# Query and key of a decoder layer's self-attention by seven half-size products, and row normalisation on ScalarE

## The chip, the core and the metric

The kernel runs on one core of a Trainium2 chip. The core has five engines with instruction queues of their own: TensorE (PE: matmuls and transposes; PEld are its weight loads), VectorE (DVE), ScalarE (ACT), GpSimd (POOL) and SyncE (SP, which issues most DMAs). Each takes its instructions in the order in which the compiler has put them; semaphores make one wait for another. The metric is the device time of one execution in microseconds (us). The kernel before took 2171.88 us, the median of three runs (2171.53 to 2173.71).

## What is computed

One decoder layer in float32, on x of 16 batches with 128 tokens (rows) and 1024 channels:

```python
x = x + self_attention(layernorm(x), Wqkv, bqkv, Wo, bo)
x = x + cross_attention(layernorm(x), ctx, ctx, Wq, Wk, Wv, Wo, bo, g)
x = x + ffn(layernorm(x), int4 weights of gate, up and down with scales and zeros)

# the part that the change touches, for each batch:
qkv = layernorm(x) @ Wqkv + bqkv             # 1024 -> q, k, v of 256 each
a = softmax(q @ k.T / sqrt(256))             # 128 x 128
x = x + (a @ v) @ Wo + bo
```

## The kernel before, in words

The program has three stages, one after the other: self-attention, cross-attention and the feed-forward network. The change lies in the first, which takes the first 250 of 2171 us. While that stage runs, DVE also prepares weights of the third: `prepare` (line 222 ff.) is a generator, named `early`, that unpacks four-bit numbers, subtracts zeros, multiplies by scales, forms sums of quarters, and has POOL issue the stores. Each `next(early)` emits one step of it; a job (one block of one matrix) is three steps, and the twelve jobs of this stage are 36 steps.

**Groups.** Self-attention works on four groups (`t` = 0 to 3) of four batches, 512 tokens each. Per group:
- *Rows.* `row_stats` (means and variances, DVE, line 144), `row_rstd` (add on DVE, power on POOL, line 150), then `turn` (line 389) for each batch: normalise 128 rows of 1024 channels (DVE, line 156), eight PE transposes into two PSUM banks (line 386), and copies into `xnT` (channels on partitions, 8 chunks of 128 channels by 512 tokens), one half by DVE (line 393), one by ACT (line 394). A group's rows are turned while the group before it multiplies. The first group's go through `first_rows`, with the normalisation on ACT already (line 169).
- *Query and key.* `query_key` (line 436): four output tiles `f` of 128 features (two of query, two of key); each is 8 matmuls, one for each chunk of channels, of 128x128 weights with 512 tokens (line 441), and ACT adds the bias on the way to `qkT` (line 450). The first group does each tile in two halves of 256 tokens.
- *Values.* `value` (line 452): for each batch, 8 matmuls of 128 tokens by 256 features (line 456), bias added by DVE (line 463).
- *Weights.* `weigh`: scores (line 471), maximum on DVE (line 479), exponentials on ACT (line 484), division on DVE (492, 493); `turn_weights`: four transposes and a copy on ACT (501, 503); `attend` (511, 514) gives `oT`.
- *Give.* For a batch of the group before, `oT` times `Wo` (line 335), added to the row `X[b]` by DVE (line 342), and the row's statistics for the next stage. `add_bias` (line 433) adds `bo` to `X[b]` on POOL.

**Order.** In the loop over `t`, each query/key tile is followed by `add_bias`, a `give`, a `turn` for the next group and one or two `next(early)`. After the four tiles come value 0, `weigh`, the other values with `turn_weights` between them, `attend`, and up to four more `next(early)`. A scheduler may let an instruction overtake others of its engine when it deems it ready. An engine wrapped in `InOrder` (line 72; its instructions all show as line 80) pins each of its instructions behind everything that was written before it on that engine; the preparation's DVE work is pinned so, other DVE work is not. In the trace, row statistics of the third group run at 31 us, long before their place in the text.

**Buffers.** PSUM: five banks named `mm` for products, three named `tr` for transposes. SBUF pools: `a_w` for weights, `a_1` with one buffer for each name, `a_2` with two (`xnT`, `xn`, `qkT`, `v`). The next stage's first loads (lines 688 to 713) wait on SP for the buffers of this stage and of the preparation.

Of the kernel before, what the change touches and what calls it, by code (L numbers as in the profile page):

```python
# [12 lines left out]
F32 = mybir.dt.float32  # L13
I32 = mybir.dt.int32
AF = mybir.ActivationFunctionType
ALU = mybir.AluOpType
# [3 lines left out]
P = 128  # L20
B, S, C = 16, 128, 1024
DH = C // 4
# [5 lines left out]
CC = C // P  # L28
NB = C // P
TB = 512  # L30
BPT = TB // S
# [52 lines left out]
def decoder_layer(  # L84
# [70 lines left out]
    def normalise(dst, src, b):  # L155
        nc.vector.tensor_scalar(
            dst, src, mv[:, b, 0:1], rstd[:, b : b + 1], ALU.subtract, ALU.mult
        )


    shift = stat.tile([P, B], F32, name="shift")

    def row_shift(b, vector):
        vector.scalar_tensor_tensor(
            shift[:, b : b + 1], mv[:, b, 0:1], -1.0, rstd[:, b : b + 1], ALU.mult, ALU.mult
        )
# [188 lines left out]
    with (  # L355
# [27 lines left out]
        def turn_half(xn, xnT, b, h):  # L383
            tr = atr.tile([P, 4, P], F32, name="tr")
            for j in range(4):
                nc.tensor.transpose(tr[:, j, :], xn[:, ts(4 * h + j, P)], ident)  # L386
            return xnT[:, ts(h, 4), ts(b % BPT, S)], tr

        def turn(b, xnT):

            xn = a2.tile([P, C], F32, name="xn")
            normalise(xn, X[b], b)
            nc.vector.tensor_copy(*turn_half(xn, xnT, b, 0))
            nc.scalar.copy(*turn_half(xn, xnT, b, 1))

        def first_rows(xnT):

            vector = InOrder(tc, nc.vector)
            halves = {}

            parts = {}

            def half(b, h):
                if h == 0:
                    parts[b] = small.tile([P, 2, 6], F32, name="bnst")
                vector.bn_stats(parts[b][:, h, :], X[b][:, ts(h, 512)])
                if h == 1:
                    vector.bn_aggr(mv[:, b, :], parts[b])
                    row_rstd(b, 1, vector)

            def rows(b):
                xn = a2.tile([P, C], F32, name="xn")
                row_shift(b, vector)
                normalise_act(xn, X[b], b)
                halves[b] = turn_half(xn, xnT, b, 0)
                nc.scalar.copy(*turn_half(xn, xnT, b, 1))

            def copy(b):
# [12 lines left out]
            copy(BPT - 1)  # L431

        def add_bias(b):
            nc.gpsimd.tensor_tensor(X[b], X[b], bo_sb, ALU.add)

        def query_key(f, xnT, qkT, ps=None, tokens=slice(None)):

            if ps is None:
                ps = aps.tile([P, TB], F32, name="mm")
            for c in range(CC):  # L440
                nc.tensor.matmul(  # L441
                    ps[:, tokens],
                    wqkv_sb[:, f, c, :],
                    xnT[:, c, tokens],
                    start=(c == 0),
                    stop=(c == CC - 1),
                )
            if tokens == ts(0, TB // 2):
                return
            nc.scalar.activation(qkT[:, f, :], ps, AF.Identity, bias=bqk_sb[:, f : f + 1])  # L450

        def value(i, xnT, v):

            ps = aps.tile([P, DH], F32, name="mm")
            for c in range(CC):
                nc.tensor.matmul(  # L456
                    ps,
                    xnT[:, c, ts(i, S)],
                    wqkv_sb[:, 4:6, c, :],
                    start=(c == 0),  # L460
                    stop=(c == CC - 1),
                )
            nc.vector.tensor_tensor(v[:, i, :], ps, bv_sb, ALU.add)

        def weigh(qkT):

            scale = 1.0 / math.sqrt(DH)
            ps = aps.tile([P, BPT, S], F32, name="mm")
            for i in range(BPT):
                for d in range(2):  # L470
                    nc.tensor.matmul(  # L471
                        ps[:, i, :],
                        qkT[:, d, ts(i, S)],
                        qkT[:, 2 + d, ts(i, S)],
                        start=(d == 0),
                        stop=(d == 1),
                    )
            nmax = small.tile([P, BPT], F32, name="nmax")
            nc.vector.tensor_reduce(nmax, ps, AX.X, ALU.max, negate=True)
            nc.scalar.mul(nmax, nmax, scale)  # L480
            at = a1.tile([P, BPT, S], F32, name="at")
            den = small.tile([P, BPT], F32, name="den")
            for i in range(BPT):
                nc.scalar.activation(
                    at[:, i, :],
                    ps[:, i, :],
                    AF.Exp,
                    bias=nmax[:, i : i + 1],
                    scale=scale,
                    accum_out=den[:, i : i + 1],  # L490
                )
            nc.vector.reciprocal(den, den)
            nc.vector.tensor_tensor(
                at, at, den.unsqueeze(2).to_broadcast([P, BPT, S]), ALU.mult
            )
            return at

        def turn_weights(at):
            tr = atr.tile([P, BPT, S], F32, name="tr")
            for i in range(BPT):  # L500
                nc.tensor.transpose(tr[:, i, :], at[:, i, :], ident)
            atT = a1.tile([P, BPT, S], F32, name="atT")
            nc.scalar.copy(atT, tr)
            return atT
# [17 lines left out]

        xnTs = [a2.tile([P, CC, TB], F32, name="xnT")]
        first_rows(xnTs[0])
        oT = None
        for t in range(NT):
            xnT = xnTs.pop()
            more = t + 1 < NT
            if more:
                xnTs.append(a2.tile([P, CC, TB], F32, name="xnT"))  # L530
                for b in range((t + 1) * BPT, (t + 2) * BPT):
                    row_stats(b)
                row_rstd((t + 1) * BPT, BPT)
            qkT = a2.tile([P, 4, TB], F32, name="qkT")
            halves = {}
            if t == 0:

                for f in range(4):
                    halves[f] = aps.tile([P, TB], F32, name="mm")
                    query_key(f, xnT, qkT, halves[f], ts(0, TB // 2))  # L540
            for f in range(4):
                if t == 0:
                    query_key(f, xnT, qkT, halves[f], ts(1, TB // 2))
                else:
                    query_key(f, xnT, qkT)
# [8 lines left out]
            v = a2.tile([P, BPT, DH], F32, name="v")  # L554
            value(0, xnT, v)
            at = weigh(qkT)
            if more:
# [4 lines left out]
                if t == 0:  # L562
                    for _ in range(3):
                        next(early)
            else:

                for i in range(1, BPT):
                    give((t - 1) * BPT + i - 1, oT)
                    value(i, xnT, v)
                    next(early, None)  # L570
                atT = turn_weights(at)
                give(t * BPT - 1, oT)
            oT = attend(atT, v)
            for _ in range((3, 3, 4, 0)[t]):
                next(early, None)
    for _ in early:
        pass
    first.close()
# [1477 lines left out]
```

## Time and profile before

| what | value |
|---|---|
| median of three runs | 2171.88 us |
| the profiled execution's own time | 2173.11 us |
| its span (first to last instruction) | 2171.3 us |
| granted TensorE clock | 0.999 of full |
| PE's share of the chain that ended last | 95% |
| first group's matmuls | from 12.55 us |
| start of group t = 1, t = 2, t = 3 | 65.47, 128.66, 191.36 us |
| first key matmul of cross-attention | 250.38 us |
| DMA while self-attention runs (0 to 300 us) | 173 GB/s |

The profile is that of one execution. A row of a timeline has the start, the length, the engine, the line, the operation, the tiles written and read, the shape and the number of instructions merged in it; behind it in brackets stands how long the engine was idle before and which operation released it. Durations of neighbours on one engine overlap a little, so that the distance from start to start is the better price of an operation in a run of them. A float32 matmul shows as two PE instructions. A row by stage has the stretch in microseconds, its length, the busy time and number of instructions of PE, PEld, DVE, ACT and POOL, the granted clock, the DMA share and GB/s. A row of waits has who waited for whom, the total, the number and the longest.

### The profile page before, as it was taken

Reading aid. Unit: us, or ns where it says so; the run is one execution under the profiler, and the core shown is the slowest. Engines: PE = TensorE matmul, PEld = TensorE weight load, DVE = VectorE, ACT = ScalarE, POOL = GpSimd, SP = SyncE. Lnnn points to the kernel's source line nnn. Section 1 sums busy time; section 2 is a strip of 40 time slices with the busy share of each in tenths; the row PEclk is TensorE's granted clock in tenths of the full one; section 3 lists DMA queues with packets and bytes.
Section 4 is the critical chain, followed back from the end, with each engine's and each line's share of the span. In section 5 each row is a group of like instructions: output and inputs, shape, how many; then the busy total and the mean of one; then the engine's idle time right before and its main releaser. Section 6 shows DMA issues by size and latency. Waiting matters only on the chain.

```text
span 2171.3 us, 25688 instructions
## 1 busy us (share of the span) xinstructions
PE 2153.8 (99%) x9004; PEld 1643.8 (76%) x9004; DVE 1556.3 (72%) x2098; ACT 525.5 (24%) x710; POOL 803.9 (37%) x675
## 2 busy tenths in 40 slices
PE   8999999999999999999999999999999999999998
PEld 7565655555555568888888888888886888888887
DVE  7899578888888758786777987878774445534573
ACT  2111235655665541211221212112111000000000
POOL 5454124333433345544444545444441022323200
PEclk9999999999999999999999999999999999999999
DMA  6446447777797676878888746677667578979941
GB/s 259 150 131 219 154 136 237 236 226 236 223 276 242 191 237 217 288 254 262 264 282 290 228 150 209 209 238 237 201 206 237 182 206 242 282 197 254 265 128 60
DMA packets 272203, 474.56 MB, mean 219 GB/s; under 512 B 29633, under 2 KB 128321, under 8 KB 266177
## 3 DMA queue, kind: packets, MB, share of 16 engines
q1 hardware_dynamic: 226736, 383.02, 54.6%
q0 software_dynamic: 27456, 71.45, 12.1%
q10 hardware_dynamic: 17872, 18.36, 2.6%
q8 instruction: 74, 1.21, 0.2%
q14 instruction: 65, 0.52, 0.1%
HBM read 314.64 MB, written 157.55 MB: 217 GB/s over the span
## 4 chain that ended last, share of the span: by engine, by line
PE 95%; DVE 3%; issue 1%; ACT 0%; POOL 0%; DMA 0%; DVEq 0%; POOLq 0%; ACTq 0%
PE q L80 38%; PE po L1929 22%; PE kq L80 10%; PE mm L80 8%; PE kx L80 5%; PE mm L441 4%; PE p L80 3%; PE mm L456 2%; PE mm L335 1%; DVE pa L80 1%; PE tr L386 0%; DVE C L80 0%; DVE pc L80 0%; PE mm L471 0%; PE mm L511 0%
## 5 line engine op out<-in xcount | busy, mean ns | idle before, releaser
L80 PE MATMUL q<-ti,li 128*128 128x256 f32 x1680 | 385.4, 379 | 0.0
L80 PEld LDWEIGHTS q<-ti,li 128*128 128x128 f32 x1680 | 319.2, 190 | 43.4
L80 ACT COPY k<-q 128x512 f32<-128x512 f32 x210 | 122.9, 585 | 660.7 <-PE q L80 645.7
L80 POOL TENSOR_TENSOR li<-w 128x512 f32<-128x512 f32 x140 | 203.8, 1461 | 52.2 <-PE q L80 31.6
L872 POOL TENSOR_TENSOR qe<-qe,qrec 128x1024 f32<-128x1024 f32 x64 | 146.2, 2284 | 175.2 <-DVE qrec L80 156.6
L80 POOL TENSOR_TENSOR li<-w,li 128x512 f32<-128x512 f32 x70 | 107.9, 1541 | 259.5 <-PE q L80 235.5
L1929 PE MATMUL po<-wc,lc 128*128 128x256 f32 x840 | 183.4, 379 | 0.0
L1929 PEld LDWEIGHTS po<-wc,lc 128*128 128x128 f32 x840 | 159.6, 190 | 21.8
L80 DVE TENSOR_TENSOR C<-q,k 128x512 f32<-128x512 f32 x150 | 102.7, 685 | 70.2 <-PE q L80 65.8
L80 PE MATMUL q<-b,w 128*128 128x256 f32 x640 | 151.2, 379 | 0.0
L80 POOL TENSOR_TENSOR li<-li,w 128x512 f32<-128x512 f32 x70 | 91.6, 1309 | 122.2 <-PE q L80 121.8
L80 PEld LDWEIGHTS q<-b,w 128*128 128x128 f32 x640 | 121.6, 190 | 17.0 <-issue 0.5
L80 PE MATMUL q<-ti,w 128*128 128x256 f32 x560 | 132.3, 379 | 0.0
L1929 PE MATMUL po<-wq,lq 128*128 128x256 f32 x560 | 126.8, 379 | 0.8 <-DVE m L80 0.8
L80 PEld LDWEIGHTS mm<-qs,m_sb 128*128 128x128 f32 x512 | 97.3, 190 | 40.1 <-issue 29.7
L80 PE MATMUL kx<-ek,cxt 128*128 128x512 f32 x256 | 121.8, 598 | 0.0
L80 DVE STREAM_TRANSPOSE kt<-qe 128x1024 f32<-128x1024 f32 x64 | 79.2, 1238 | 58.8 <-POOL qe L872 54.6
L80 PE MATMUL mm<-qs,m_sb 128*128 128x256 f32 x512 | 120.8, 379 | 0.0
L80 PE MATMUL kq<-wq_sb,xn 128*128 128x512 f32 x256 | 120.2, 593 | 0.4 <-ACT qe L860 0.4
L80 PE MATMUL kq<-wk_sb,cx 128*128 128x512 f32 x256 | 120.1, 592 | 0.0
L1929 PEld LDWEIGHTS po<-wq,lq 128*128 128x128 f32 x560 | 106.0, 190 | 16.7 <-DVE m L80 1.2
L80 DVE TENSOR_TENSOR pa<-pa,sz 128x1024 f32<-128x1024 int32 x86 | 116.4, 1354 | 2.1
(203 smaller groups left out, 3712.2 us busy)
## 6 DMA issues: line engine op xcount, KB each, us to landing
ti<-r SPq DMA_DIRECT2D x36, 1024.0 KB, 7.4
w<-wg SPq DMA_DIRECT2D x140, 256.0 KB, 3.3
w<-wu SPq DMA_DIRECT2D x140, 256.0 KB, 3.8
lq<-h SPq DMA_DIRECT2D x140, 256.0 KB, 5.3
kd<-kt SPq DMA_DIRECT2D x62, 512.0 KB, 3.7
qs<-kd SPq DMA_DIRECT2D x244, 128.0 KB, 3.2
h<-h SPq DMA_DIRECT2D x80, 256.0 KB, 3.1
wq<-wd SPq DMA_DIRECT2D x70, 256.0 KB, 7.4
```

What stands on the lines that cost most here:

```text
L80: return lambda *args, **kw: self._tc.keep_in_program_order(fn(*args, **kw))
L335: tensor.matmul(ps, oT[:, d, ts(b % BPT, S)], wo_d[d][:, ts(h, 512)], start=(d == 0), stop=(d == 1),)
L441: nc.tensor.matmul(ps[:, tokens], wqkv_sb[:, f, c, :], xnT[:, c, tokens], start=(c == 0), stop=(c == CC - 1),)
L456: nc.tensor.matmul(ps, xnT[:, c, ts(i, S)], wqkv_sb[:, 4:6, c, :], start=(c == 0), stop=(c == CC - 1),)
L872: nc.gpsimd.tensor_tensor(qe, qe, rec.unsqueeze(2).to_broadcast(wide), ALU.mult)
L1929: nc.tensor.matmul(bank[:, i, :], l[:, ts(i, S)], w,  start=(start and c == 0 and i % 2 == 0), stop=(stop and c == len(pairs) - 1), skip_g ...
```

## The change

*Seven products.* For the second to fourth group, the product of query/key weights and rows is cut in two along output features (query, key), channels (chunks 0 to 3, 4 to 7) and tokens (256 and 256). Eight products of quarters are replaced by seven of sums and differences of quarters (the Winograd form of Strassen's method). `weight_sums` makes three sums of weight quarters (S1, S2, S4) once, in the first group, and overwrites a fourth quarter by a difference: four DVE operations of 128x1024, pinned in order. For each group, DVE makes the differences of tokens T1, T2, T3 and a second form of T2, four of 128x1024; T3 overwrites a quarter of `xnT` (in the last group it has a tile of its own). Products 6, 5 and 3 are added on top of product 1 in its PSUM bank, and product 4 on top of product 7. Between, ACT copies partial sums with the bias to `qkT` (8 of 128x256 in place of 4 of 128x512), and DVE adds three of 128x512.

*Order.* Values of batches 2 and 3 come ahead of the products (value 0 too), value 1 after them. Two of the four pieces of work for the neighbouring groups (`beside`) go between products, two after `weigh`; in the last group all four go between products. The steps of `early` by group are 5, 10, 10, 11 in place of 6, 9, 12, 9.

*Rows.* `turn` normalises on ACT (which needs `shift`, made for four batches in one DVE instruction) and copies both halves on ACT. Row statistics are written one group earlier.

*Buffers.* `qkT` and `v` have one buffer; the softmax's tile shares one with T1; S1, S2 and S4 are new.

The diff, cut to its core:

```diff
     def turn(b, xnT):
         xn = a2.tile([P, C], F32, name="xn")
-        normalise(xn, X[b], b)
-        nc.vector.tensor_copy(*turn_half(xn, xnT, b, 0))
-        nc.scalar.copy(*turn_half(xn, xnT, b, 1))
+        normalise_act(xn, X[b], b)
+        for h in range(2):
+            nc.scalar.copy(*turn_half(xn, xnT, b, h))
...
-            at = a1.tile([P, BPT, S], F32, name="at")
+            at = a1.tile([P, 2 * BPT, S], F32, name="T1")[:, :BPT]
...
+        HALF, HC = TB // 2, CC // 2
+        S1, S2, S4 = (aw.tile([P, 2, HC, P], F32, name=f"S{n}") for n in (1, 2, 4))
+        def outputs_by_inputs(m, kc):
+            return wqkv_sb[:, ts(m, 2), ts(kc, HC)]
+        def weight_sums():
+            A = outputs_by_inputs
+            for dst, a, b, op in (
+                (S1, A(1, 0), A(1, 1), ALU.add),
+                (S2, S1, A(0, 0), ALU.subtract),
+                (S4, A(0, 1), S2, ALU.subtract),
+                (A(1, 0), A(0, 0), A(1, 0), ALU.subtract),
+            ):
+                InOrder(tc, nc.vector).tensor_tensor(dst, a, b, op)
+        def query_key_products(xnT, qkT, own=None):
+            A = outputs_by_inputs
+            def rows(kc, th):
+                return xnT[:, ts(kc, HC), ts(th, HALF)]
+            T1 = a1.tile([P, 2 * BPT, S], F32, name="T1").rearrange("p (c h) s -> p c (h s)", c=HC)
+            T2 = a1.tile([P, HC, HALF], F32, name="T2")
+            T3 = rows(0, 1) if own is None else own
+            nc.vector.tensor_tensor(T1, rows(0, 1), rows(0, 0), ALU.subtract)
+            nc.vector.tensor_tensor(T2, rows(1, 1), T1, ALU.subtract)
+            L = {1: A(0, 0), 2: A(0, 1), 4: A(1, 1), 7: A(1, 0), 5: S1, 6: S2, 3: S4}
+            R = {1: rows(0, 0), 2: rows(1, 0), 3: rows(1, 1), 4: T2, 5: T1, 6: T2, 7: T3}
+            bank = {}
+            def biased(m, th, ps):
+                for n in range(2):
+                    f = 2 * m + n
+                    nc.scalar.activation(
+                        qkT[:, f, ts(th, HALF)], ps[:, n], AF.Identity, bias=bqk_sb[:, f : f + 1]
+                    )
+            def add(m, th, ps):
+                dst = qkT[:, ts(m, 2), ts(th, HALF)]
+                nc.vector.tensor_tensor(dst, ps, dst, ALU.add)
+            def third():
+                nc.vector.tensor_tensor(T3, rows(1, 1), rows(0, 1), ALU.subtract)
+            def product(p):
+                first = {6: 1, 5: 1, 3: 1, 4: 7}.get(p, p)
+                if p == first:
+                    bank[p] = aps.tile([P, 2, HALF], F32, name="mm")
+                ps = bank[first]
+                for n in range(2):
+                    for c in range(HC):
+                        nc.tensor.matmul(
+                            ps[:, n],
+                            L[p][:, n, c],
+                            R[p][:, c],
+                            start=(p == first and n == c == 0),
+                            stop=(p in (2, 3, 4) and c == HC - 1),
+                            skip_group_check=True,
+                        )
+                if p == 1:
+                    biased(0, 0, ps)
+                elif p == 7:
+                    biased(1, 1, ps)
+                elif p == 6:
+                    biased(1, 0, ps)
+                    nc.vector.tensor_tensor(T2, rows(1, 0), T2, ALU.subtract)
+                elif p == 2:
+                    add(0, 0, ps)
+                elif p == 5:
+                    add(1, 1, ps)
+                elif p == 4:
+                    add(1, 0, ps)
+                else:
+                    biased(0, 1, ps)
...
+            def beside(f, between=lambda: None):
                 add_bias(t * BPT + f)
+                if t + 2 < NT:
+                    row_stats((t + 2) * BPT + f)
                 if more:
                     if oT is not None:
                         give((t - 1) * BPT + f, oT)
+                    between()
                     turn((t + 1) * BPT + f, xnTs[0])
                 if t > 0:
-                    for _ in range(2 if t == 2 else 1 + f % 2):
+                    for _ in range((3, 2, 2, 2)[f] if more else 2):
                         next(early, None)
...
+            else:
+                for i in (2, 3) if more else ():
+                    value(i, xnT, v)
+                third()
+                value(0, xnT, v)
+                for f, ps in enumerate(((1, 7), (6, 2), (5, 4), (3,))):
+                    for p in ps:
+                        product(p)
+                    if f < 2 or not more:
+                        beside(f)
+                    elif f == 2:
+                        next(early)
+                value(1, xnT, v)
+                at = weigh(qkT)
+                if more:
+                    beside(2)
+                    turned = []
+                    beside(3, lambda: turned.append(turn_weights(at)))
+                    atT = turned.pop()
```

More of the change, by code (lines that the diff above doesn't have):

```diff
@@ L153, in row_rstd, with row_shift @@
         gpsimd.tensor_tensor(r, r, mhalf[:, :n], ALU.pow)
[L155 to L158, printed above, removed]
     shift = stat.tile([P, B], F32, name="shift")
[L163 removed]
+    def row_shift(b, vector, n=1):
         vector.scalar_tensor_tensor(
[L165 removed]
+            shift[:, b : b + n], mv[:, b : b + n, 0], -1.0, rstd[:, b : b + n], ALU.mult, ALU.mult
         )
@@ new lines, in query_key_products @@
+        def query_key_products(xnT, qkT, own=None):
[51 more added lines that the diff above has]
+                    biased(0, 1, ps)
+            return product, third
@@ L528, in decoder_layer @@
             more = t + 1 < NT
+            qkT = a1.tile([P, 4, TB], F32, name="qkT")
+            if t > 0:
+                own = None
+                if not more:
+                    own = a2.tile([P, CC, TB], F32, name="xnT")[:, :HC, :HALF]
+                product, third = query_key_products(xnT, qkT, own)
             if more:
                 xnTs.append(a2.tile([P, CC, TB], F32, name="xnT"))
-                for b in range((t + 1) * BPT, (t + 2) * BPT):
+                for b in range(BPT, 2 * BPT) if t == 0 else ():
                     row_stats(b)
                 row_rstd((t + 1) * BPT, BPT)
[L534 to L545, printed above, removed]
+                row_shift((t + 1) * BPT, nc.vector, BPT)
+            def beside(f, between=lambda: None):
                 add_bias(t * BPT + f)
+                if t + 2 < NT:
+                    row_stats((t + 2) * BPT + f)
                 if more:
@@ L549, in decoder_layer @@
                         give((t - 1) * BPT + f, oT)
+                    between()
                     turn((t + 1) * BPT + f, xnTs[0])
                 if t > 0:
-                    for _ in range(2 if t == 2 else 1 + f % 2):
+                    for _ in range((3, 2, 2, 2)[f] if more else 2):
                         next(early, None)
[L554 to L557, printed above, removed]
+            v = a1.tile([P, BPT, DH], F32, name="v")
+            if t == 0:
+                halves = {}
+                for f in range(4):
+                    halves[f] = aps.tile([P, TB], F32, name="mm")
+                    query_key(f, xnT, qkT, halves[f], ts(0, HALF))
+                for f in range(4):
+                    query_key(f, xnT, qkT, halves[f], ts(1, HALF))
+                    beside(f)
+                value(0, xnT, v)
+                at = weigh(qkT)
+                weight_sums()
                 value(1, xnT, v)
@@ L561, in decoder_layer @@
                 value(3, xnT, v)
-                if t == 0:
-                    for _ in range(3):
-                        next(early)
[L565 to L572, printed above, removed]
+                for _ in range(3):
+                    next(early)
[3 more added lines that the diff above has]
+                third()
+                value(0, xnT, v)
+                for f, ps in enumerate(((1, 7), (6, 2), (5, 4), (3,))):
+                    for p in ps:
+                        product(p)
+                    if f < 2 or not more:
+                        beside(f)
+                    elif f == 2:
+                        next(early)
+                value(1, xnT, v)
+                at = weigh(qkT)
+                if more:
[3 more added lines that the diff above has]
+                    atT = turned.pop()
+                else:
+                    for i in range(1, BPT):
+                        give((t - 1) * BPT + i - 1, oT)
+                        if i > 1:
+                            value(i, xnT, v)
+                        next(early, None)
+                    atT = turn_weights(at)
+                    give(t * BPT - 1, oT)
             oT = attend(atT, v)
-            for _ in range((3, 3, 4, 0)[t]):
-                next(early, None)
+            if t == 0:
+                for _ in range(2):
+                    next(early)
     for _ in early:
```

## The prediction

> **What bounds the kernel now.** I read the page first, then busy time by stage, then the order of time inside self-attention.
>
> ```profile
> PE 2153.8 (99%) x9004; PEld 1643.8 (76%) x9004; DVE 1556.3 (72%) x2098; ACT 525.5 (24%) x710; POOL 803.9 (37%) x675
> ```
>
> TensorE (PE) is busy 99% of the span, and the chain that ended last is PE for 95%. A microsecond of PE work saved is a microsecond of time, if nothing takes PE's place. So I looked at what else is nearly full in the changed stage. The next rows give, for the first group, the second and third, the fourth, and the rest of the kernel, the length and the busy time of PE, weight loads, VectorE (DVE), ScalarE (ACT) and GpSimd (POOL):
>
> ```profile
> 12.55:65.47 52.92, 52.91 (x277) 47.21 (x278) 34.91 (x52) 11.55 (x24) 27.19 (x13) 1.00 0.50 188
> 65.47:191.36 125.89, 125.49 (x459) 75.42 (x458) 119.03 (x182) 17.11 (x40) 60.57 (x68) 1.00 0.49 159
> 191.36:250.38 59.02, 59.02 (x198) 34.36 (x197) 50.35 (x80) 6.21 (x16) 19.28 (x35) 1.00 0.61 202
> 250.38:2171.00 1920.62, 1912.58 (x8062) 1483.67 (x8060) 1344.73 (x1769) 485.66 (x626) 694.53 (x551) 1.00 0.72 223
> ```
>
> In groups two and three (the first with t = 1 and t = 2) DVE is busy 119.0 of 125.9 us: 95%. PE hardly notices: its only wait on DVE in the whole stage is
>
> ```profile
> PE mm L511 <- DVE v L463: 0.4, 1, 0.4
> ```
>
> Both engines are full there; this decides the case. ACT has 108 us to spare in the same stretch. The granted clock is 1.00 in all rows.
>
> **PE: what the seven products save.** One group's query and key are 64 PE instructions (32 matmuls, two instructions each) 512 wide. The fourth group has them in one piece in the chain; the first group's halves give the price of the 256-wide form, here in the order of time:
>
> ```profile
> 191.52 27.47 PE mm L441 x64
> ```
> ```profile
> 34.54 3.62 PE L441 MATMUL mm<-xnT,wqkv_sb 128*128 128x256 f32 x16
> 37.99 1.04 PE L386 MATMUL tr<-ident,xn 128*128 128x128 f32 x8
> ```
>
> Before: 27.47 us, 429 ns each. Sixteen 256-wide ones take 37.99 - 34.54 = 3.45 us, 215.6 ns each: half the width at half the time, the weight load (190 ns) still under it. After: 7 products x 2 output tiles x 4 chunks = 56 matmuls, 112 instructions x 215.6 = 24.15 us. Saved: 3.32 us a group, **9.96 us** for three. The other end: the page's widest use of this form (L80 q<-ti,li, 385.4 us for 1680) is 229 ns with the waits in it; 112 x 229 = 25.7 saves 5.4 in all. I take 9.96, because the operands here come from SBUF long before, as in the first group's row.
>
> The Trainium skill ("TensorE: Matmul & The Clock Gate", Back-to-back issue gap) speaks against narrower matmuls: it gives sustained spacings of about 131 ns at 512 columns and 81 at 128, so the time falls much less than the width. Interpolated, 256 would cost about 0.75 of 512, an estimate from that page, and 112 instructions would cost 1.3 times the 64: some 8 us more a group. The rows above say 0.502, and the sum goes by them.
>
> The other PE work is moved, not changed: values two and three come first (so that the in-place difference may overwrite their tokens), value 0 next, value 1 last.
>
> **DVE: what it loses and gains.** Prices are start to start, where DVE ran without a break. Normalise 0.72 (85.41 to 86.13), copy of transposes 0.60 (110.43 to 111.03), 1024-wide tensor_tensor 1.13 (113.02 to 114.15), PSUM add 0.59 (102.88 to 103.47). A weight-preparation job of three steps runs from 192.53 to 201.58, so one next(early) is 3.0 us.
> - Groups two and three lose 8 copies (4.8) and the 6 normalises in that stretch (4.3): -9.1.
> - Each group with products gains four token differences (4.5), three adds (1.8) and a row_shift (0.1): 6.4, for two 12.8. T1 and T2 of group two need only tokens that are ready early; DVE idles 3.03 and 3.47 us in front of the first group's last two value adds, and four weight sums (4.5) and these two (2.3) nearly fit there. So +10.5.
> - next(early): 5, 10, 10, 11 by group, against a load in the trace of 8 jobs (24 steps) between 65.47 and 191.36. After: 25 steps, +3.0. The fourth group loses one, -3.0.
>
> DVE's demand in groups two and three: 119.0 - 9.1 + 10.5 + 3.0 = 123.4 us, and PE needs only 125.9 - 6.6 = 119.3. It is **4.1 us short**. In the fourth: 50.35 + 6.3 - 3.0 = 53.7 against 59.0 - 3.3 = 55.7: 2.0 to spare. So relieving DVE of rows pays for the differences, and PE's new pace does the rest.
>
> **The new waits.** Product 3 is summed into the bank that add(1,1) has to read first on DVE; only product 4 (3.45 us of PE) lies between. Queued behind the waiting PE instruction are value 1, the scores and the softmax, so the group. How late DVE serves such an operation today is read from the two copies of one pair of transposes, one half on idle ACT, the other on DVE:
>
> ```profile
> 76.84 0.59 ACT L394 COPY xnT<-tr 128x512 f32<-128x512 f32 x1 [3.62 <-PE tr L386]
> ...
> 82.26 0.64 DVE L393 COPY xnT<-tr 128x512 f32<-128x512 f32 x1
> ```
>
> DVE is 5.4 us later: preparation steps and row statistics stand ahead of it. The other seven pairs differ by 4.3, 4.3, 0.1, 2.2, 3.4, 3.8 and 1.7. With 0.6 for the add, what exceeds 3.45 is 2.55, 1.45, 1.45, 0, 0, 0.55, 0.95, 0: 0.87 a group, **2.6 us** for three. This and the shortage are largely the same lateness, so they bound the loss: 2.6 at least, 4.1 + 2.6 = 6.7 if both are paid. I take the shortage less the 2.0 spare, plus 0.6 a group at product 3: 4.1 - 2.0 + 1.9 = **4.0**.
>
> Costed at nothing, with the cover:
> - The normalises and second copies on ACT: 4 x (1.24 + 0.585) = 7.3 us a group, and eight half-wide bias adds for four (0.69 each at full width; between 0.37, the 128-wide exponential, and 0.69: 0.2 to 2.8 us more). ACT would be busy about 35 of 119 us. The transposes' rows come from it while PE does give's 3.44 us; a normalise behind two bias adds is 2.6 after product 7. Without that cover, 1.2 a batch.
> - T3 for product 7: behind value 0 and product 1, 6.9 us. T2's second form: 11 us ahead of product 4. Softmax: before, 6.9 us of values covered it; now two gives and a turn, 7.75.
> - The row_shift for four batches waits on POOL's power, and DVE stands behind it: so did normalise (1.16 us in front of it at 125.51). Zero to 1.2 a group, taken as zero.
> - The weights turned to attend: value 3's 3.45 us of cover becomes one turn, 0.87. Turn to copy's end is 0.63 + 0.58 (59.68, 60.31), against 0.43 + 0.87 on PE: just enough; up to 1.2 with a normalise in front.
> - The add_biases on POOL stay. They stretch DVE: preparation's tensor_scalar is 614 ns in groups two and three and 420 in the fourth, where POOL adds nothing. This is in the 119.0.
>
> **The end of the stage.** The next stage's loads queue in order on SP behind preparation's last product, and cx behind value 3:
>
> ```profile
> 242.15 0.80 SPq L690 DMA_DIRECT2D cxt<-in_cxt  x2
> ...
> 244.92 0.33 SPq L688 DMA_DIRECT2D cx<-in_cx  x1
> ```
>
> PE uses them from 250.38; cx lands 3.7 after issue, so 1.7 us are left. DVE may end 4 us later against PE before this costs; I take zero, with up to 3 as the other end. From there the rest is PE's (1912.6 of 1920.6), so what is saved by 250 is kept.
>
> **Sum.** 2173.1 (the profiled execution; span 2171.3) - 9.96 + 4.0 = 2167.1. It was 1.2 above the median of the three runs, 2171.88, so against that **2165.9**. A measurement of this kernel tells about 0.2%, 4.3 us, from no change.
>
> **Rivals.**
> 1. *Nothing given back* (14%). For it: ACT takes work off the crowded engine, the preparation only fills, and PE waited 0.4 us in all with DVE at 95%. Against: that was with 7 us free. -9.96: 2161.9.
> 2. *DVE becomes the bound and eats it* (29%). For it: 123.4 against 119.3, and five steps of the first group that now start behind the weight sums. Both losses in full, 6.7, and 1 to 3 at the next stage's loads: -1.3, 2170.6; "within 0.2%".
> 3. *Slower* (15%). One mechanism: preparation keeps its written place behind every earlier DVE instruction, and add(1,1) stands behind the two steps written before it (6.0), give's adds and statistics (2.7) and a stretched step. If it lands about 9.5 us after product 5, PE stands 6 us in each of three groups: 18 - 10 = +8, 2180. It decides above 3.3 us a group (add(1,1) 6.8 after product 5); slower beyond 0.2% from 4.8. Against: value adds and maxima overtake preparation in today's order (nmax at 181.81, between two of its steps).
> 4. That the products don't shorten PE at all is the 229 ns case at worst, still -5.4, and lies inside the others.
>
> The forecast (-4.3 to -8) has 42%, with the first rival 56% faster; 29% the same; 15% slower. The range runs from the full gain to 2174, past the second rival; the third is left out.
>
> **What will show it.** Right: 112 instructions of 128x256 a group at 215 to 216 ns; PE idle of 1 to 2 us a group ahead of product 3, released by the add on DVE; DVE over 97% in groups two and three; the first key matmul of cross-attention some 6 us earlier. Wrong: PE idle ahead of products 7 or 4 (differences late), ahead of transposes (ACT late), or at the first key matmul with an SP load as releaser; above all a wait of over 3 us at product 3.

## The result and the profile after

The changed kernel takes 2177.23 us (median of 17 runs, 2174.90 to 2178.76), the kernel before in the same sessions 2173.02 (17 runs, 2171.22 to 2174.44). The ratio is 1.0021, 95% interval [1.0015, 1.0028]: slower by 4.2 us. The profiled execution has a span of 2175.5 us, against 2171.3 before. The forecast was 6.0 us faster in the profile's own terms.

The engine row of the page looks harmless. PE does 6.7 us less work than before, and still the time is longer:

```profile
PE 2147.1 (99%) x9148; PEld 1671.9 (77%) x9148; DVE 1547.0 (71%) x2102; ACT 546.7 (25%) x746; POOL 796.7 (37%) x675
```

So PE must stand still or run slowly somewhere. The busy time by stage shows where (columns as before: stretch, length, PE, PEld, DVE, ACT, POOL, clock, DMA share, GB/s). Rows one and two are groups two and three, and group four; then come two short stretches that did not exist before, and the rest:

```profile
66.11:188.00 121.89, 119.14 (x555) 93.57 (x554) 107.90 (x170) 28.98 (x62) 52.14 (x65) 1.00 0.47 154
188.00:245.24 57.24, 56.31 (x246) 43.29 (x244) 56.93 (x92) 6.83 (x20) 21.53 (x37) 1.00 0.63 208
245.24:253.00 7.76, 0.00 (x1) 0.01 (x1) 2.03 (x5) 0.59 (x1) 1.26 (x3) 0.78 1.03 400
253.00:256.46 3.46, 3.44 (x4) 1.50 (x5) 0.31 (x3) 0.00 (x0) 0.00 (x0) 0.51 0.67 194
258.21:2175.00 1916.79, 1909.16 (x8053) 1482.11 (x8051) 1342.12 (x1763) 484.41 (x624) 693.56 (x550) 1.00 0.72 222
```

Groups two to four took 125.89 + 59.02 = 184.91 us before and take 121.89 + 57.24 = 179.13 now: 5.8 us are won, almost the 6.0 of the forecast. Then PE does nothing for 7.8 us, and for 3.46 us more its granted clock is 0.51. The order of time names the releaser:

```profile
243.30 1.95 PE L506 MATMUL mm<-atT,v 128*128 128x128 f32 x16
253.02 5.35 PE L80 MATMUL kq<-wk_sb,cx 128*128 128x512 f32 x8 [7.78 <-DMA cx<-in_cx]
258.21 1.88 PE L80 MATMUL kx<-ek,cxt 128*128 128x512 f32 x4
```

The first eight key matmuls of cross-attention wait for the first context batch, and take 258.21 - 253.02 = 5.19 us, 1.75 more than the 3.44 before, where PE came to them without a wait:

```profile
250.38 3.60 PE L80 MATMUL kq<-wk_sb,cx 128*128 128x512 f32 x8
253.82 1.88 PE L80 MATMUL kx<-ek,cxt 128*128 128x512 f32 x4
```

Sum from the second group's start: -5.8 + 7.8 + 1.75 = +3.75. The second group starts 0.64 later (in the fourteen profiles of this study that start scatters from 63.8 to 66.5 us, and kernels with and without the products overlap), the rest of the kernel is 0.2 shorter: together the spans' +4.2.

The load that PE waits for stands in SP's queue, here in the changed kernel, in order of time:

```profile
239.66 0.33 SPq L810 DMA_DIRECT2D wo_again<-in_wo  x1
240.48 0.33 SPq L792 DMA_DIRECT2D cxt<-in_cxt  x1
240.86 0.42 SPq L810 DMA_DIRECT2D wo_again<-in_wo  x1
241.34 0.42 SPq L805 DMA_DIRECT2D wk_sb<-in_xwk  x1
241.81 0.46 SPq L790 DMA_DIRECT2D cx<-in_cx  x1
```

Before, the context batch came fourth, at 244.92, ahead of both output weights:

```profile
245.29 0.92 SPq L708 DMA_DIRECT2D wo_again<-in_wo  x2
```

Now both of these, needed only later, are ahead of it. It is issued 3.1 us earlier than before, and lands 3.1 us later: 11.1 us after its issue, while the DMA engines move 400 GB/s. The DMA rows of before and after for this one load (the last number is the time from issue to landing):

```profile
cx<-in_cx SPq DMA_DIRECT2D x1, 512.0 KB, 4.9
```
```profile
cx<-in_cx SPq DMA_DIRECT2D x1, 512.0 KB, 11.1
```

In the changed kernel the first `wo_again` waited on SP for the last group's value 3, and the other loads stood behind it:

```profile
SPq L810 <- PE mm L451: 14.3, 1, 14.3
```

By the order and sizes of the pools (argued from the program; no trace shows addresses), its buffer lies in the new layout where `xnT` was. With one buffer for `qkT` instead of two, and new tiles beside it, everything behind had moved; in the layout before, the place was that of `qkT` and its neighbours.

Inside the stage the waits of PE are few (who waits on whom, total, times, longest):

```profile
PE kq L80 <- DMA cx<-in_cx: 7.8, 1, 7.8
PE mm L573 <- DVE qkT L561: 2.7, 2, 1.7
PE mm L573 <- ACT qkT L555: 0.9, 1, 0.9
```

### The profile page after: what moved, and what is told of

Same layout as the page of the kernel before. It is cut to its first block, busy times and chain, and to the rows that moved or that the text cites. A ratio compares the mean times of both kernels' runs of the same rounds, so it can differ in the third digit from the quotient of the medians.

```text
span 2175.5 us, 26039 instructions
## 1 busy us (share of the span) xinstructions
PE 2147.1 (99%) x9148; PEld 1671.9 (77%) x9148; DVE 1547.0 (71%) x2102; ACT 546.7 (25%) x746; POOL 796.7 (37%) x675
## 3 DMA queue, kind: packets, MB, share of 16 engines
q8 instruction: 75, 1.23, 0.2%
## 4 chain that ended last, share of the span: by engine, by line
PE 93%; DVE 4%; issue 1%; DMA 1%; ACT 0%; SPq 0%; POOL 0%; DVEq 0%; ACTq 0%; POOLq 0%
PE q L80 38%; PE po L2031 22%; PE kq L80 10%; PE mm L80 8%; PE kx L80 5%; PE p L80 3%; PE mm L451 2%; PE mm L436 1%; DVE pa L80 1%; PE mm L573 1%; PE mm L330 1%; DMA cx<-in_cx 1%; DVE pc L80 0%; PE tr L381 0%; DVE bnst L147 0%
## 5 line engine op out<-in xcount | busy, mean ns | idle before, releaser
L80 PEld LDWEIGHTS q<-ti,w 128*128 128x128 f32 x560 | 106.4, 190 | 14.5
```

Source lines behind the costliest of these rows:

```text
L80: return lambda *args, **kw: self._tc.keep_in_program_order(fn(*args, **kw))
```

## The experiments

The theory: the products win about 6 us in the stage as forecast; the order of the loads, which comes from the buffers' layout, takes 9.5 (7.8 of wait, 1.75 of slow clock). Rivals: the in-stage gain is not what it seems and DVE or ACT takes it back at the stage's end; or moving rows to ACT is itself the loss. Ratios are to the kernel before on the same chip. "Stage" means the time from the second group's first matmul to the first key matmul in the profile (184.91 before, 186.91 changed).

**The loads in the written order.** The changed kernel, with the ten loads from `wk_sb` to the second context pinned on SP as written:

```diff
-        nc.sync.dma_start(wk_sb, xwk)
-        ctxs = {batches[0]: load_ctx(batches[0])}
+        sync.dma_start(wk_sb, xwk)
+        ctxs = {batches[0]: load_ctx(batches[0], sync)}
...
-            nc.sync.dma_start(wo_again[d], wo[ts(d, P)])
+            sync.dma_start(wo_again[d], wo[ts(d, P)])
```

> The changed kernel; only the ten loads of the next stage are pinned on SP in the order of their first use: wk_sb, cx, cxt, then wo_again and the rest. Theory (the gain of 5.1 us inside self-attention is lost because cx lands 7.8 us late behind 1 MB of wo_again, and PE then runs 3.5 us at half its clock): the wait at the first key matmul falls below 1 us, no half clock, and the time is that of the kernel before less about 5: ratio 0.9975, some 9 us under the changed kernel. Rival (the DMA engines are full of preparation's stores and any 3 MB of loads take this long; another load becomes the late one): PE waits 5 us or more at some other load within 20 us, ratio 1.000 to 1.002.

Measured: 2167.82 us, ratio 0.9974 [0.9965, 0.9984]; 9.4 us below the changed kernel. The context batch is issued at 239.20 and lands 3.3 later; PE goes on without a wait:

```profile
242.88 1.95 PE L506 MATMUL mm<-atT,v 128*128 128x128 f32 x16
244.66 3.65 PE L80 MATMUL kq<-wk_sb,cx 128*128 128x512 f32 x8
248.14 1.88 PE L80 MATMUL kx<-ek,cxt 128*128 128x512 f32 x4
```

The waits inside the stage stay (2.8 and 0.9), the stage takes 179.00. The loss against the kernel before lies wholly in the order of the loads. This is the base ("pinned kernel") of what follows.

**The layout alone.** The kernel before, without products; only `qkT` and `v` get a pool of their own ahead of `xnT`'s, so that the first output weights come to lie under `xnT`:

```diff
+        tc.tile_pool(name="a_q", bufs=2) as aq,
...
-            qkT = a2.tile([P, 4, TB], F32, name="qkT")
+            qkT = aq.tile([P, 4, TB], F32, name="qkT")
...
-            v = a2.tile([P, BPT, DH], F32, name="v")
+            v = aq.tile([P, BPT, DH], F32, name="v")
```

> The kernel before; qkT and v only stand in a pool of their own ahead of xnT and xn, so that the last group's xnT lies under the buffer of the first wo_again. Nothing else is changed. Theory (where the buffers lie sets SP's order of the loads): wo_again goes ahead of cx, cx lands 4 to 8 us after PE wants it at 250.4, and PE runs at half clock after that: ratio 1.002 to 1.005, without any of the seven products. Rival (the lateness comes from the products' work on DVE and the stores behind it): no wait, ratio 1.000.

Measured: 2179.87, ratio 1.0035 [1.0021, 1.0048]. The order of SP's queue and PE's answer:

```profile
245.38 0.81 SPq L709 DMA_DIRECT2D wo_again<-in_wo  x2
246.23 0.43 SPq L704 DMA_DIRECT2D wk_sb<-in_xwk  x1
246.70 0.43 SPq L689 DMA_DIRECT2D cx<-in_cx  x1
```
```profile
255.49 5.37 PE L80 MATMUL kq<-wk_sb,cx 128*128 128x512 f32 x8 [4.53 <-DMA cx<-in_cx]
260.69 1.88 PE L80 MATMUL kx<-ek,cxt 128*128 128x512 f32 x4
```

The same turn of the order, the wait and the slow clock, with no product in the kernel. Where buffers lie is enough to turn the order.

**Control: the kernel before, pinned** (the same edit of the loads on it).

> The kernel before with the same ten loads pinned in the written order: nothing of the products. PE waited for no load there, so if the pinned order was worth 9.4 us only because the change had disturbed the order, this gives a ratio of 1.000 (within 0.001). If the pinned order is an improvement that any kernel here would take, it is faster than before by 2 us or more, and part of the pinned kernel's gain over before isn't the products'.

Measured: 2173.60 beside 2173.59, ratio 0.9999 [0.9990, 1.0008]; stage 184.92. The pinned order is worth nothing by itself, so the pinned kernel's 5.5 us below before are the products' and rows'.

**Output weights first, in the pinned kernel.** Only the place of these two loads changes, to ahead of `wk_sb`; then the exact order of the changed kernel, with `cxt` between them:

```diff
+            sync.dma_start(wo_again[d], wo[ts(d, P)])
+            if d == 0:
+                sync.dma_start(ct, cxt[batches[0]])
+        sync.dma_start(wk_sb, xwk)
+        sync.dma_start(c, cx[batches[0]])
```

(The first of the two runs has no `if`, and loads `cxt` behind `cx`.)

> The pinned kernel with one thing changed in the pinned order: both loads of the output projection's weights stand ahead of the key weights and the first context batch instead of behind them. If that place in SP's queue is what costs, the wait for the context batch at the first key matmul is back (5 to 8 us), with the key matmuls at a lower clock behind it, and the ratio is 1.001 to 1.002, as the changed kernel's. If the pinned kernel won by something else (all ten loads issued in one block, or the preparation's loads kept behind them), it stays at 0.997 to 0.998.

> The pinned kernel with the exact order in which the changed kernel's loads stood: output weights, context's other copy (cxt), output weights, key weights, context batch. With both output weights alone ahead the wait was 3.1 us. If the rest of the 7.8 us is the cxt load between them (512 KB, at the 400 GB/s of this stretch 1.3 us alone, more beside the preparation's stores), the wait is 6 to 8 us, the key matmuls take 5.2 us, and the ratio is 1.0015 to 1.0025, as the changed kernel's. If something else than these five loads' order made it (the later loads, the layout itself), the wait stays near 3 us and the ratio at 1.000.

Measured: 2172.04, ratio 0.9996 [0.9987, 1.0005], and 2177.56, ratio 1.0016 [1.0007, 1.0026]. The first key matmuls of the one and of the other:

```profile
248.42 5.37 PE L80 MATMUL kq<-wk_sb,cx 128*128 128x512 f32 x8 [3.09 <-DMA cx<-in_cx]
```
```profile
251.84 5.97 PE L80 MATMUL kq<-wk_sb,cx 128*128 128x512 f32 x8 [6.65 <-DMA cx<-in_cx]
```

The first was expected to wait 5 to 8 us and to be at 1.001 to 1.002; it is half as bad. The output weights explain 3.1 us of wait and the slow clock, and the `cxt` load between them most of the rest: 6.65 of 7.78. The key matmuls took 5.97 us there, 0.8 more than expected, since the clock stayed low for longer. The last microsecond of the wait is not explained; the preparation's stores share the DMA engines then.

**Rows alone.** The kernel before, with `turn` normalising and copying on ACT as in the change (and `row_shift` for four batches, which this needs):

```diff
-            normalise(xn, X[b], b)
-            nc.vector.tensor_copy(*turn_half(xn, xnT, b, 0))
-            nc.scalar.copy(*turn_half(xn, xnT, b, 1))
+            normalise_act(xn, X[b], b)
+            for h in range(2):
+                nc.scalar.copy(*turn_half(xn, xnT, b, h))
```

> The kernel before with the rows of the second to fourth group normalised by ScalarE and both halves of the transposes copied by it; query and key by the old products. Theory (this part only relieves DVE, on which PE hardly waits): ratio 1.000 within 0.0007; DVE busy some 9 us less between 65 and 191 us. Rival (ScalarE's longer normalise of 1.24 us comes late for the transposes): PE waits before transposes, ratio 1.001 or more.

Measured: 2172.76, ratio 0.9998 [0.9989, 1.0007]. DVE's busy time in groups two and three falls from 119.0 to 113.4 us (5.6, where some 9 were expected), PE has no wait from the second group on, and the time does not move: relief of an engine that nobody waits for.

**Products without the rows' move.** The pinned kernel with rows on DVE as before (the same lines the other way).

> As the run with the loads in order, but the rows are normalised and half copied by DVE as in the kernel before. Theory (DVE has 14 us of forced idle in groups two and three, but its order puts preparation ahead of the adds): the waits of PE ahead of product 3 grow to 2 to 4 us a group, 3 to 8 us slower than the run with the loads in order, ratio 0.999 to 1.001. Rival (the relief of DVE is not needed): the same time as the run with the loads in order within 1 us.

Measured: 2175.17, ratio 1.0012 [1.0003, 1.0021], 7.35 us above the pinned kernel. The waits came at other places than I expected, not at product 3:

```profile
PE mm L575 <- DVE T L549: 4.5, 1, 4.5
PE mm L453 <- DVE mv L148: 2.7, 1, 2.7
PE kq L80 <- ACT oT L511: 0.7, 1, 0.7
```

T2 is late for product 6 of the last group, and a value of the third group stands behind DVE. Behind each of the two longer waits the granted clock falls (0.60 and 0.59 over 3.4 and 3.5 us). The rows' move is worth nothing alone and 7 us to the products, as long as the loads are in order.

**No row sums.** The pinned kernel with T1, T2 and T3 replaced by plain quarters of `xnT`. It leaves out four DVE sums a group (the two below, T3 and T2's second form), so its query and key are not the layer's:

```diff
-            nc.vector.tensor_tensor(T1, rows(0, 1), rows(0, 0), ALU.subtract)
-            nc.vector.tensor_tensor(T2, rows(1, 1), T1, ALU.subtract)
+            T1, T2, T3 = rows(0, 1), rows(1, 1), rows(0, 1)
```

> The pinned kernel without the four sums of rows in each of the three groups (T1, T2, T3 and the later T2): the products take the rows as they are, so that 4 DVE instructions of 1.2 us a group, 14.4 us in all, go, and the query and key are not the reference's. If the 4 us that the three groups lose against the products' 9.96 us are DVE's demand, the waits at product 3 and at product 6 go and it is 3 to 4 us faster than the pinned kernel (about 0.9957 of before). If they are the order on DVE (preparation ahead of the sum of products 1 and 5), the waits at product 3 stay and it is within 1 us of the pinned kernel.

Measured: 2161.76, ratio 0.9948 [0.9935, 0.9962]. No wait is left from the second group on, the stage takes 174.83:

```profile
63.77:238.60 174.83, 174.81 (x798) 137.08 (x797) 157.55 (x251) 35.78 (x82) 73.36 (x101) 1.00 0.54 178
```

That is 10.08 below before, the 9.96 of the prediction within 0.12. The 4.2 us between this and the pinned kernel are DVE's new work, which is what the first expectation says. It goes a little beyond the 3.7 us of waits.

**Two ways to shorten those waits.** First, the preparation's steps moved out from ahead of the sum that product 3 waits for:

```diff
-                    for _ in range((3, 2, 2, 2)[f] if more else 2):
+                    for _ in range((3, 0, 3, 3)[f] if more else 2):
```

> The kernel with its loads pinned in order, and in each group with a successor the preparation's steps dealt 3, 0, 3, 3 instead of 3, 2, 2, 2, so that none stands between product 7's row sums and the sum of products 1 and 5, which product 3 waits for. If the steps ahead of that sum hold product 3, its two waits (1.0 and 1.8 us) go and the median falls by 2 to 3 us below that of the pinned kernel (0.9974 of before), to about 0.996. If DVE is short in sum, or the adds of the output projection hold it, the waits stay or turn up at another instruction and the ratio stays at 0.997.

Measured: 2176.72, ratio 1.0017 [1.0008, 1.0026]. Both theories missed. The waits did turn up elsewhere, as the second says, but they are nearly three times as long in all:

```profile
PE tr L381 <- ACT xn L164: 4.6, 1, 4.6
PE mm L573 <- DVE T L547: 1.7, 1, 1.7
PE mm L573 <- DVE qkT L561: 1.4, 2, 1.0
PE mm L506 <- DVE v L458: 1.3, 1, 1.3
```

The first comes from DVE and POOL together. The fourth group's rows need an addition on DVE (line 152) and a power of four numbers on POOL. The addition runs at 136.38, 72.2 us after the second group's start; in the pinned kernel this was 68.2 (133.85), so DVE is 4.0 us later. Then POOL has to finish a power of one number, 0.65 us in the pinned kernel, and six stores behind it, 3.5 us more:

```profile
130.11 6.80 POOL L153 TENSOR_TENSOR rstd<-rstd,mhalf 128x1 f32<-128x1 f32 x1
136.87 2.17 POOL L229 DMA_DIRECT2D wu<-pc  x4
139.04 1.07 POOL L229 DMA_DIRECT2D wg<-pa  x2
140.12 1.04 POOL L153 TENSOR_TENSOR rstd<-rstd,mhalf 128x4 f32<-128x4 f32 x1
```

The shift on DVE, the normalise on ACT and the transposes follow from there. That the steps bunched is my reading of DVE's rows, with no run of its own. Why the one power takes ten times as long (DVE runs without a break beside it) was not tried by itself.

Second, PE work put between the sum and its waiter: the pinned kernel with value 1 ahead of product 3.

```diff
                 for f, ps in enumerate(((1, 7), (6, 2), (5, 4), (3,))):
+                    if f == 3:
+                        value(1, xnT, v)
                     for p in ps:
                         product(p)
...
-                value(1, xnT, v)
                 at = weigh(qkT)
```

> The pinned kernel with the values' product of the second batch row issued ahead of product 3 instead of behind it: 8 matmuls of 215 ns (1.7 us of PE) stand between the sum of products 1 and 5 and its waiter. If only the time of that sum counts, the waits of 1.0 and 1.8 us at product 3 shrink to 0 and 0.1, and the median falls by about 2.5 us below that of the pinned kernel, to 0.9963 of before. If the softmax is late instead, since nothing follows product 3 at once, the transposes of the weights wait by as much as was won, and the ratio stays at 0.997.

Measured: 2166.11, ratio 0.9965 [0.9952, 0.9979]. Product 3 waits no more (0.9 us for ACT, 0.3 for T3 and 0.7 ahead of the key matmuls remain), the transposes aren't late, and the stage takes 177.22, 1.8 less than the pinned kernel's. By the intervals the two can't be told apart; the profile shows the wait gone. It is the fastest kernel of the study that computes everything: 11 to 12 us below the changed one, 7.5 below before.

**Is the slow clock the idleness?** The changed kernel with matmuls of no use (the unit matrix by itself) on PE while it waits for the context batch, 60 and then 30:

```diff
+                idle = aps.tile([P, P], F32, name="idle", tag="mm")
+                for n in range(60):
+                    InOrder(tc, nc.tensor).matmul(idle, ident, ident, start=True, stop=True)
```

> The changed kernel, loads as the change leaves them, with 60 matmuls of 128x128 without use (the unit matrix by itself, 111 ns each by the transposes' row, 6.7 us in all) on PE between the last attend and the first key matmul, inside the 7.8 us that PE waits for the context batch. If PE's idleness is what lowers the granted clock behind the wait, the eight key matmuls take 3.4 to 3.7 us instead of 5.2 at a granted clock near 1.0, the wait that is left is about 1 us, and the median is 1.7 us below that of the changed kernel (ratio 1.0013 instead of 1.0021). If the clock falls for another reason (the transfers at over 400 GB/s at that time), the key matmuls stay at 5.2 us and nothing is won.

> The changed kernel with 30 matmuls without use instead of 60 ahead of the first key matmul: the 60 took 13.6 us (two records of 111 ns each), so 30 should take 6.8 us of the 7.8 that PE waits. If PE's idleness lowers the clock, about 1 us of wait is left, the eight key matmuls take 3.4 to 3.7 us at a granted clock near 1.0, and the ratio is 1.0013 (1.7 us below the changed kernel's 1.0021). If the clock had stayed up behind the 60 only because the transfers were over by then, the key matmuls take 5.2 us again and the ratio is 1.002.

Measured: 2180.89, ratio 1.0034 [1.0021, 1.0048], and 2180.66, ratio 1.0031 [1.0019, 1.0044]. The 60 are two records each and took 13.4 us, longer than the wait, a mistake of mine in the size. The key matmuls of the run with 30, and what follows:

```profile
253.31:256.79 3.48, 3.48 (x8) 1.41 (x8) 0.17 (x2) 0.00 (x0) 0.00 (x0) 1.00 0.38 93
259.18:262.12 2.94, 2.94 (x4) 1.16 (x5) 0.00 (x0) 0.86 (x1) 0.00 (x0) 0.61 0.03 13
```
```profile
245.22 6.86 PE L80 MATMUL idle<-ident 128*128 128x128 f32 x60
253.31 3.67 PE L80 MATMUL kq<-wk_sb,cx 128*128 128x512 f32 x8 [1.23 <-DMA cx<-in_cx]
259.18 3.16 PE L80 MATMUL kx<-ek,cxt 128*128 128x512 f32 x4 [2.19 <-ACT ek L898]
```

With PE kept busy the eight key matmuls run at full clock in 3.48 us: idleness is what lowers it. The other reading, that the transfers do, is ruled out by the stretch of the 30 matmuls themselves: the DMA engines move 400 GB/s as in the changed kernel's wait, and the granted clock (third number from the end) is 1.00:

```profile
245.20:252.08 6.88, 6.88 (x62) 6.69 (x60) 2.21 (x6) 0.59 (x1) 1.45 (x3) 1.00 1.01 400
```

The gain didn't reach the time. In this build ACT has a row's normalisation in front of the exponential of the keys, the next matmuls wait 2.19 us for that, and behind this new gap the clock falls again (0.61). So the forecast of 1.0013 failed, by a wait that the changed kernel doesn't have. Why ACT's order differs is not shown; the run with the exact order of the changed kernel's loads has the same order on ACT, without the 30 matmuls, and waits 0.73 us there.

## Why the prediction was wrong

The step that failed is "The end of the stage", which I took at zero with up to 3 us: it cost 9.5. I asked there only how late DVE might be. I took for granted that SP's queue would keep its order, with the context batch ahead of the output weights, and did not ask which buffers these loads lie in, although the change's list of buffers (one `qkT` in place of two, new tiles) says that they move. I also read the slack too wide: the DMA rows of before give 4.9 us from issue to landing for this load, not 3.7, so it landed at 249.8, 0.55 us ahead of its use and not 1.7 (3.7 is the time of the second context batch, 12 us later). And I priced only the wait, not the clock behind it. My list of what would show it wrong did name the place, "at the first key matmul with an SP load as releaser".

Point by point:
- *PE's saving, 9.96 us*: right. Sixteen instructions of 128x256 take 91.14 - 87.69 = 3.45 us, 215.6 ns each:

```profile
87.69 3.62 PE L573 MATMUL mm<-T,S 128*128 128x256 f32 x16
91.14 3.62 PE L573 MATMUL mm<-xnT,wqkv_sb 128*128 128x256 f32 x16
```

  and without DVE's sums the stage is 10.08 us shorter. The other end (229 ns) and the rule of the Trainium skill that I weighed against this ("TensorE: Matmul & The Clock Gate", Back-to-back issue gap: time falls much less than width, some 8 us more a group by my estimate) did not come about.
- *The loss inside the stage, 4.0 us*: right in size; 184.91 - 179.00 = 5.91 kept of 9.96 in the pinned kernel is a loss of 4.05. That the two agree so well is luck, since the 4.0 came from a shortage of DVE in sum that was not there (next point; and three times 0.6 is 1.8, so the terms add up to 3.9). Its parts were off: waits at product 3 of 1.0 and 1.75 and none in the last group (forecast 1 to 2 each), and 0.9 for ACT's half-wide bias at product 6, which I had at nothing. That DVE's new work is behind it is shown by the run without row sums. PE's order counts too: value 1 ahead of product 3 gave 1.8 us back with the same work on DVE.
- *DVE's demand*: wrong by 12 us. Forecast for groups two to four 123.4 + 53.7 = 177.1, measured 107.9 + 56.9 = 164.8: 15.5 less in groups two and three, 3.2 more in the fourth. The preparation in groups two and three took 72.3 us instead of 83.6, where I had added 3.0. Half a job fewer ran there, and most of its instructions were shorter (30 of 614 ns became 30 of 449, the 1024-wide ones fell from 1397 to 1284 ns). I had put the 614 down to the `add_bias` on POOL, but six of these run there before and after, so they alone don't explain it; what does is open. DVE isn't over 97% busy there but 89%; 11.5 of its 14 idle us are spent waiting for PE ahead of the output projection's adds, with the pinned preparation behind them. It is full in the last group, 56.93 of 57.24 us. So it is short at places, not in sum.
- *The rows' move pays for the differences*: right in effect; 7.35 us without it, nothing alone.
- *The slower rival* (steps ahead of the sum hold product 3 for 6 us) did not come about: the longest wait there is 1.75 us. The kernel is slower by another mechanism than the one I had named.
- *From there the rest is PE's, and what is saved is kept*: right only with the loads in order; the pinned kernel's stage is 5.91 shorter and its time 5.5. In the changed kernel 9.5 were lost at the passage.

## What to carry to other kernels

A change that alters tiles in one stage moves the buffers of the next stage's loads, and so their order in the queue: before you count a gain at a stage's end, list the first loads behind it with their buffers, who frees these, and how much slack the first user has. Where an order matters, pin it; here that cost nothing on the old kernel and gave back 9.4 us on the new one. And price a PE wait of more than about 2 us with the slow clock behind it.

## What the runs showed of the hardware

Behind a wait the granted clock fell to a half. It fell behind waits of 7.78, 6.65, 4.64, 4.54, 4.53, 3.09, 2.66 and 2.19 us, and in the kernel with the steps dealt anew behind 1.27 and 0.67 us within 2.7 us of each other; it did not behind 1.73 to 1.75 us (seven profiles) and 1.23 us. The fall comes with a delay. In the run with the output weights first PE had waited from 245.33 to 248.42, worked on at full clock for 0.9 us, and only then did the clock fall to 0.50, for some 3.4 us:

```profile
248.90:249.30 0.40, 0.40 (x2) 0.19 (x1) 0.00 (x0) 0.00 (x0) 0.00 (x0) 1.00 0.89 358
249.70:250.20 0.50, 0.50 (x2) 0.03 (x1) 0.00 (x0) 0.00 (x0) 0.00 (x0) 0.50 1.06 422
253.00:253.60 0.60, 0.60 (x2) 0.19 (x1) 0.00 (x0) 0.00 (x0) 0.00 (x0) 1.00 0.88 263
```

In the two longest waits it fell inside the wait, some 4.4 us after its start, and stayed at a half for 6.8 us in all, 3.4 (changed kernel) and 4.6 (its exact order, pinned) of them over the key matmuls. These took 1.75 us more than at full clock behind 3.09 us of wait as behind 7.78, and 2.5 more behind 6.65: the price doesn't follow the length of the wait.

The Trainium skill ("TensorE: Matmul & The Clock Gate", HAM oscillation — how this bites in real kernels) has PE gated down behind gaps of more than some 3.4 us; the 3.4 us that the low clock lasts agree with its window, but the gap that suffices was shorter here.
